# Nine diffusions instead of six ahead of the first blocks, in one step of a graph network's third layer

## The chip, the cores and the metric

The kernel runs on one core of a Trainium2 chip. The metric is the device time of one execution in microseconds (us). The engines are TensorE (PE: matmuls and transposes), VectorE (DVE), ScalarE (ACT), GpSimd (POOL) and SyncE (SP, which here only issues DMAs). Each engine works through its own queue in order; semaphores hold an instruction until what it needs is there.

## The reference

Four graph layers run one after the other on 4096 nodes with 256 features each, and all of them use one 0/1 adjacency matrix `adj` (4096 x 4096). After each layer the result is added to its input and normalised. Only layer 2 matters here. It does the following, cut to what is needed:

```python
R = S + eye(N);  R = R / R.sum(-1, keepdims=True)      # S is adj
Z = 0;  Xf = X;  Xa = X
for n in range(2):                                      # two steps
    A = top_p_attention(Xa, W1, W2, W3)                 # softmax, cut to the nucleus of 0.9
    Xf = R @ Xf                                         # diffusion
    Xa = A @ Xa                                         # attention
    Z = Z + Xf @ U1[n].T + Xa @ U2[n].T
h = X + Z                                               # then layer norms
```

`top_p_attention` forms the scores `q @ k.T` of all pairs of nodes, takes the softmax of each row, and keeps of each row the largest probabilities whose sum, before each, is under 0.9 (the nucleus).

## The kernel before, in words

The 4096 rows are worked in 32 blocks of 128 (NB = 32). Each of the two steps of layer 2 has the same parts, all in the function `layer2`:

- `keys` transposes the features and makes queries and keys; `spreads` computes, row by row, the quantities from which a first guess of the nucleus's threshold is made.
- `scores(b)` (L904) makes the scores of block b on PE in chunks and ACT exponentiates them (L886) into one of three buffers `e0`, `e1`, `e2`, taken in turn, each 128 x 4096. DVE adds up the partial sums (L912). As there are three buffers, block b + 3 overwrites block b, once block b's attention has transposed it.
- `guessed(e, b, ...)` (L915) is mostly ACT: from the sum it guesses a threshold (L929), and for blocks from 2 on ACT counts above it in four passes (L955); out of this come the corrected threshold `c2` (L894) and others.
- `nucleus(...)` (L969) is DVE: it starts at L1003 with `c2`, counts above the threshold with `evaluate` (L901; two counts in the second step, one in the first) and corrects it each time with help of ACT (L985 to L997), then sweeps the row (L1033), takes the largest values (L1037), finds the cut, and writes zeros below it: the edges (L1084, eight instructions).
- `attention(dst, e, r)` (L1209) is PE: 32 transposes (L1215), which ACT copies out of PSUM (L1217), and 32 products with the features (L1220).
- `diffusion(step, b)` (L1234) calls `diffuse`: 33 matmuls (L153, L159) into the PSUM tile `ps_r`, of which there is one buffer, with eight loads of adjacency pieces of 256 KB each by SP into five buffers. ACT (L1229) and DVE (L1230) scale the sum out of PSUM.
- `close(step, b, two)` (L1254) multiplies diffusion and attention with the weights (`terms`: PE L1250, DVE L1252), and in the second step normalises the rows, for which DVE (L80, L81, L1270, L1271, L1274), POOL (L83, L84) and ACT (L894) take turns. In the second step `ahead3` then computes what layer 3 needs of the block (PE L1284).

Before the loop over the blocks, each step runs `scores(0)`, `guessed`, the nucleus of block 0, and then EARLY = 6 diffusions, of blocks 0 to 5, whose results ACT stores in DRAM (`ahead`, L1320). The scores of blocks 1 and 2 come in between. In the loop, iteration b does the attention and the close of block b, the scores and guess of block b + 2, the nucleus of block b + 1, and obtains the diffusion of block b + 1: read back from DRAM by SP (L1326) where it was computed ahead, else computed there.

This is the order in the program's text. A scheduler then sets the order of each engine's queue, by priority, when the kernel is built; instructions of several blocks are interleaved in each queue. That order is fixed when the kernel runs.

Of the kernel before, what the change touches and what calls it, by code (L numbers as in the profile page):

```python
# [46 lines left out]
def row_broadcast(v, n):  # L47

    return bass.AP(tensor=v.tensor, offset=v.offset, ap=[[0, P], [1, n]])


class Net:
# [653 lines left out]
    def layer2(self):  # L706
        nc, tc, NB, D, X, N = self.nc, self.tc, self.NB, self.D, self.X, self.N
        A = 64
        HALF = N // 2
        with ExitStack() as ctx:  # L710
# [143 lines left out]
            def spreads(mom, qs, qg):  # L854

                for g in range(NB // 4):
                    pg = psum.tile([P, 512], F32, name="ps_tp")
                    for q in range(4):
                        b = 4 * g + q
                        s = b * P // 512 % 2  # L860
                        other = slice((1 - s) * A, (2 - s) * A)
                        nc.tensor.matmul(pg[:, q * P:(q + 1) * P], qs[other, b * P:(b + 1) * P], mom[other, :P],
                                         start=True, stop=True)
                    pg = pg.rearrange("p (q m) -> p q m", q=4)
                    t = qg[:, g % 4 * 256:g % 4 * 256 + 256].rearrange("p (q m) -> p q m", q=4)
                    nc.scalar.copy(t, pg[:, :, :A])
                    nc.vector.tensor_mul(t, t, pg[:, :, A:])
                    nc.vector.tensor_reduce(hvar[:, 4 * g:4 * g + 4], t, AX.X, ALU.add)
                nc.vector.tensor_scalar_max(hvar, hvar, 1e-6)
                nc.scalar.activation(lnr, hvar, AF.Ln)  # L870
                nc.scalar.activation(spread, lnr, AF.Exp, scale=0.5)
                nc.scalar.activation(lnr, lnr, AF.Identity, scale=0.5, bias=cs[:, 0:1])
                nc.vector.tensor_scalar(hvar, hvar, 0.5, -0.7, op0=ALU.mult, op1=ALU.add)
                nc.vector.tensor_scalar_add(qsp, spread, QUANTILE[-1])
# [29 lines left out]
            def scores(b):  # L904

                q = work.tile([P, P], F32, name="q", bufs=2)
                nc.sync.dma_start(q, qd[:, b * P:(b + 1) * P])
                e = es[b % 3][:, :N]
                zp = small("zp", HALF // 512)
                product(q, e, sums=zp)  # L910
                Z = Zs[:, b:b + 1]
                nc.vector.tensor_reduce(Z, zp, AX.X, ALU.add)  # L912
                return e
# [295 lines left out]
            def attention(dst, e, r):  # L1209
                pa = ps1.tile([P, 512], F32, name="ps_a")  # L1210
                for g in range(NB // 4):
                    pt = psum.tile([P, 512], F32, name="ps_tp")
                    for k in range(4):
                        jc = 4 * g + k
                        nc.tensor.transpose(pt[:, k * P:(k + 1) * P], e[:, jc * P:(jc + 1) * P], self.ident)  # L1215
                    aT = work.tile([P, 512], F32, name="aT", bufs=2)
                    nc.scalar.copy(aT, pt)  # L1217
                    for k in range(4):
                        jc = 4 * g + k
                        nc.tensor.matmul(pa[:, :D], aT[:, k * P:(k + 1) * P], X[:, jc, :],  # L1220
                                         start=(jc == 0), stop=(jc == NB - 1))
                nc.scalar.mul(dst, pa[:, :D], r)
# [6 lines left out]
                nc.scalar.mul(dst, pr[:, D:], rdeg[:, at(b)])  # L1229
                nc.vector.scalar_tensor_tensor(dst, pr[:, :D], rdeg[:, at(b)], dst, op0=ALU.mult, op1=ALU.add)  # L1230

            EARLY = min(6, NB)

            def diffusion(step, b):  # L1234

                dif = work.tile([P, 1, D], F32, name="dif")
                diffuse(dif[:, 0], b)
                if step == 0:
                    part = work.tile([P, 2, D], F32R, name="part", bufs=1)
                    self.split(part, dif[:, 0])  # L1240
                    nc.scalar.dma_start(xfd[b], part.bitcast(F32))
                return dif
# [36 lines left out]
            def ahead3(b, h, last=False):  # L1279

                pz = ps1.tile([P, 512], F32, name="ps_r")
                xT = self.transposed(psum, work, h, "xT")
                for c in range(2):
                    nc.tensor.matmul(pz, xT[:, c, :], w3[:, c].rearrange("p k m -> p (k m)"),  # L1284
                                     start=(c == 0), stop=(c == 1))
                if last:
                    self.split(XD[:, b], pz[:, D:])
                else:
                    part = work.tile([P, 2, D], F32R, name="part", bufs=1)
                    self.split(part, pz[:, D:])  # L1290
                    nc.scalar.dma_start(xfd[at(b)].rearrange("o p s d -> (o p) s d"), part.bitcast(F32))
                nc.scalar.copy(h[:, 0], pz[:, :D])
                nc.scalar.dma_start(xo[at(b), :, 1].rearrange("o p d -> (o p) d"), h[:, 0])

            for step in range(2):
                if step == 1:
                    for b in range(0, NB, 4):
                        nc.sync.dma_start(X[:, b:b + 4, :], xad[b:b + 4].rearrange("b p d -> p b d"))
                for i, ut in enumerate((self.u1t, self.u2t)):
                    nc.scalar.dma_start(u[:, i], ut[step].rearrange("(c p) m -> p c m", p=P))  # L1300
                nc.scalar.dma_start(affine, row_broadcast((self.ln_b, self.ln_g)[step], D))

                nc.scalar.preload_act_table_set("natural_log_exp_and_others")
                found = keys(X)
                if step == 1:
                    for k in range(2):
                        nc.scalar.dma_start(w3[:, :, k], self.w3[k * D:(k + 1) * D].rearrange("(c p) m -> p c m", p=P))
                if step == 0:
                    for b in range(NB):
                        self.split(XD[:, b], X[:, b, :])  # L1310
                e = scores(0)
                spreads(*found)
                stage = {0: guessed(e, 0, ABOVE[step])}
                rs = {0: nucleus(*stage[0], evals=1 + step)}
                difs = {}

                for k in range(EARLY):
                    if k in (2, 4):
                        stage[k // 2] = guessed(scores(k // 2), k // 2, ABOVE[step])
                    nc.scalar.dma_start(ahead[k], diffusion(step, k)[:, 0])  # L1320

                def diffused(b):
                    if b >= EARLY:
                        return diffusion(step, b)
                    dif = work.tile([P, 1, D], F32, name="dif")
                    nc.sync.dma_start(dif[:, 0], ahead[b])  # L1326
                    return dif

                difs[0] = diffused(0)
                for b in range(NB):  # L1330
                    if b + 1 < NB:
                        rs[b + 1] = nucleus(*stage[b + 1], evals=1 + step) if b == 0 else None
                    last = b == NB - 1
                    e, r = stage.pop(b)[0], rs.pop(b)
                    if last:
                        if step == 1:
                            ahead3(b - 1, h)
                        mend(step, e, r)

                        n = NB - step  # L1340
                        for k in range(0, n, 4):
                            to = min(k + 4, n)
                            nc.sync.dma_start(XD[:, k:to].bitcast(F32), xfd[k:to].rearrange("b p s d -> p b s d"))
                    att = work.tile([P, 1, D], F32, name="att", bufs=1)
                    attention(att[:, 0], e, r)
                    if step == 1 and 0 < b < NB - 1:
                        ahead3(b - 1, h)
                    h = close(step, b, (difs.pop(b), att))
                    if step == 1 and last:
                        ahead3(b, h, last)  # L1350
                    if 3 <= b + 2 < NB:
                        stage[b + 2] = guessed(scores(b + 2), b + 2, ABOVE[step])
                    if b + 1 < NB:
                        if b:
                            rs[b + 1] = nucleus(*stage[b + 1], evals=1 + step)
                        difs[b + 1] = diffused(b + 1)
# [114 lines left out]
```

## Time and profile before

| | |
|---|---|
| time, median of 10 runs | 4506.37 us (4500.6 to 4509.62) |
| the profiled execution's own time | 4505.58 us |
| its span in the profile | 4503.9 us |
| busy in the span: PE / DVE / ACT / POOL | 94% / 74% / 61% / 7% |
| layer 2's second step, from its first count on DVE to its last close | 2949.7 to 4236.2 us |
| block 0's attention begins on PE | 3008.3 us |
| block 9's attention begins on PE | 3336.9 us |
| block 30's attention begins on PE | 4157.7 us |

All times inside the run are counted from the start of the span. A wait "A <- B" is idle time of A's engine just before A, put down to B, whose end came last. In the lists in order of time, "x8" is the number of instructions merged in one line; a product of 32-bit numbers counts twice.

### The profile page before, as it was taken

To read this page: it belongs to the slowest core of one execution; us is meant where nothing else is said; L and a number is where in the kernel's file an instruction comes from. 1 tells how busy PE (TensorE), PEld (TensorE's weight loads), DVE (VectorE), ACT (ScalarE), POOL (GpSimd) and SP (SyncE) were. 2 spreads that over 40 slices of the span, in tenths; PEclk is the share of its full clock that TensorE was granted. 3 is DMA by queue.
4 is the path that set the end of the run, shared out by engine and by line. 5 is a ranking of instruction groups with operands and counts; after the bars stand their busy time and mean duration, and the time that the engine had idled before them with its cause. 6 is when DMAs were issued, how large, how long until landed. Compare 5 with 4: busy or idle time off the path is not lost. (4 is left out here: it accounts for less than half of the span.)

```text
span 4503.9 us, 70573 instructions
## 1 busy us (share of the span) xinstructions
PE 4244.9 (94%) x25625; PEld 3414.7 (76%) x25625; DVE 3344.6 (74%) x7657; ACT 2762.2 (61%) x5501; POOL 315.4 (7%) x538
## 2 busy tenths in 40 slices
PE   8999989999997999999999999887999999999799
PEld 7899989999986876677777767665666666666587
DVE  7632259999994446977777777388989999989354
ACT  5533369998873235866666666257677777676232
POOL 0111100001102100000000000001000000000011
PEclk9999999999998999999999999999999999999899
DMA  4765553342215964022222222530122222222541
GB/s 132 222 198 178 177 201 105 96 140 64 85 39 200 385 237 142 26 75 87 81 79 80 79 81 87 197 119 30 39 79 76 80 79 80 67 70 77 190 141 47
DMA packets 277781, 523.51 MB, mean 116 GB/s; under 512 B 36774, under 2 KB 112294, under 8 KB 273318
## 3 DMA queue, kind: packets, MB, share of 16 engines
q1 hardware_dynamic: 179268, 356.20, 23.7%
q10 hardware_dynamic: 85282, 122.62, 8.0%
q0 software_dynamic: 12864, 39.99, 3.0%
q8 instruction: 207, 3.39, 0.3%
q14 instruction: 160, 1.31, 0.1%
HBM read 363.63 MB, written 155.06 MB: 115 GB/s over the span
## 5 line engine op out<-in xcount | busy, mean ns | idle before, releaser
L1220 PE MATMUL ps_a<-X,aT 128*128 128x256 f32 x4096 | 960.1, 386 | 29.0 <-ACT aT L1217 28.4
L1220 PEld LDWEIGHTS ps_a<-X,aT 128*128 128x128 f32 x4096 | 760.2, 190 | 293.8 <-ACT aT L1217 141.2
L272 PE MATMUL acc<-gm,gt 128*128 128x198 bf16 x8192 | 710.2, 250 | 38.5 <-issue 17.9
L272 PEld LDWEIGHTS <-gt 128*128 128x128 fp8e4 x8192 | 705.2, 98 | 43.5 <-issue 18.0
L264 ACT ACTIVATE sg<-lpb,nlc 128x1024 fp8e4<-128x1024 f32 x640 | 671.1, 1139 | 78.9 <-DVE gt L266 39.0
L479 PE MATMUL pz<-src,ar 128*128 128x264 f32 x4096 | 510.4, 287 | 11.7 <-DVE ar L469 8.6
L479 PEld LDWEIGHTS pz<-src,ar 128*128 128x128 f32 x4096 | 506.6, 189 | 15.3 <-DVE ar L469 13.2
L159 PE MATMUL ps_r<-XD,adj_piece 128*128 128x512 f32 x2048 | 508.2, 400 | 10.1 <-DMA adj_piece<-adjs 9.9
L1217 ACT COPY aT<-ps_tp 128x512 f32<-128x512 f32 x512 | 277.8, 584 | 355.4 <-PE ps_tp L1215 350.4
L955 ACT ACTIVATE ja<-e,nc 128x2048 uint8<-128x2048 f32 x240 | 479.2, 1997 | 0.5 <-issue 0.2
L882 PE MATMUL ps_logit<-kT,q 64*128 64x512 f32 x1024 | 462.5, 637 | 4.0 <-ACT e L886 3.9
L159 PEld LDWEIGHTS ps_r<-XD,adj_piece 128*128 128x128 f32 x2048 | 382.9, 190 | 108.2 <-DMA adj_piece<-adjs 22.1
L901 DVE SCALAR_TENSOR_TENSOR v<-e,c 128x4096 bf16<-128x4096 f32 x100 | 447.3, 4473 | 7.3 <-ACT c L929 6.5
L1037 DVE MAX8 cand<-v 128x8 f32<-128x256 f32 x1024 | 360.9, 413 | 2.2
L1084 DVE SCALAR_TENSOR_TENSOR e<-e,edge 128x512 f32<-128x512 f32 x512 | 347.4, 747 | 1.5
L182 ACT ACTIVATE adj_piece<-na 128x1024 fp32r<-128x1024 fp8e4 x128 | 135.4, 1061 | 327.3 <-PE ps_adj L695 134.7
L472 ACT ACTIVATE nb<-a 128x512 uint8<-128x512 f32 x256 | 156.9, 632 | 292.4 <-DMA a<-in_adjt_dram 281.0
L1215 PE MATMUL ps_tp<-ident,e 128*128 128x128 f32 x2048 | 273.5, 275 | 39.2 <-DVE e L1084 26.1
L1033 DVE SCALAR_TENSOR_TENSOR v<-e,hi 128x2048 f32<-128x2048 f32 x128 | 301.0, 2351 | 1.7
L1215 PEld LDWEIGHTS ps_tp<-ident,e 128*128 128x128 f32 x2048 | 242.5, 142 | 78.0 <-DVE e L1084 29.5
L886 ACT ACTIVATE e<-ps_logit 128x1024 f32<-128x1024 f32 x256 | 261.4, 1022 | 48.5 <-PE ps_logit L882 33.6
L257 DVE TENSOR_SCALAR sg<-lpb,nlc 128x1024 fp8e4<-128x1024 f32 x384 | 274.2, 752 | 1.7
(301 smaller groups left out, 5093.4 us busy)
## 6 DMA issues: line engine op xcount, KB each, us to landing
adj_piece<-adjs SPq DMA_DIRECT2D x512, 256.0 KB
a<-in_adjt_dram SPq DMA_DIRECT2D x256, 256.0 KB
adjs<-adj_piece SPq DMA_DIRECT2D x128, 512.0 KB
na<-nad SPq DMA_DIRECT2D x64, 512.0 KB
na<-nad ACTq DMA_DIRECT2D x32, 1024.0 KB
nad<-nb POOLq DMA_DIRECT2D x128, 128.0 KB, 3.4
lpb<-lpd POOLq DMA_DIRECT2D x32, 512.0 KB, 4.2
xfd<-part ACTq DMA_DIRECT2D x63, 256.0 KB
```

The lines of the kernel that those rows point to most:

```text
L159: nc.tensor.matmul(ps, a[:, k, :], rhs(jc).rearrange("p s d -> p (s d)"), start=(jc == 0 and own is None), stop=(jc == self.NB - 1))
L264: nc.scalar.activation(sg[:, k, :], lpb, AF.Sign, scale=-1.0, bias=nlc[:, jc, h:h + 1], saturate=False)
L272: nc.tensor.matmul(acc[:, q, :6 * C1], gt[:, k, q * P:(q + 1) * P], gm[:, jc, hh, :], start=(jc == 0 and q % 2 == 0), stop=(jc == NB - 1 a ...
L479: nc.tensor.matmul(pz[q][:, t, :W], ar[:, q, k, :], src[:, jc, t, s], start=(jc == 0 and s == 0), stop=(jc == NB - 1 and s == 1))
L882: nc.tensor.matmul(pl[:, s, :], q[s * A:(s + 1) * A, :], kT[s * A:(s + 1) * A, c * 512:(c + 1) * 512], start=True, stop=True)
L901: nc.vector.scalar_tensor_tensor(junk, e, c, e, op0=ALU.is_ge, op1=ALU.mult, accum_out=S)
L955: nc.scalar.activation(ja, e[:, s * HALF:(s + 1) * HALF], f, bias=nc1, accum_out=fs[:, i + s:i + s + 1])
L1033: nc.vector.scalar_tensor_tensor(v, ec, hi, ec, op0=ALU.is_lt, op1=ALU.mult, accum_out=sb[:, s:s + 1])
L1037: nc.vector.max(cand[:, 8 * j:8 * j + 8], v[:, k * 256:(k + 1) * 256])
L1084: nc.vector.scalar_tensor_tensor(ec, ec, edge[:, j:j + 1], ec, op0=ALU.is_ge, op1=ALU.mult)
L1215: nc.tensor.transpose(pt[:, k * P:(k + 1) * P], e[:, jc * P:(jc + 1) * P], self.ident)
L1220: nc.tensor.matmul(pa[:, :D], aT[:, k * P:(k + 1) * P], X[:, jc, :], start=(jc == 0), stop=(jc == NB - 1))
```

## The change

In the second step nine diffusions (blocks 0 to 8) are made ahead of the block loop, not six (blocks 0 to 5). The first step keeps its six. The store to and the reload from DRAM go with each of the three; the loop no longer computes diffusions 6, 7 and 8.

```diff
-            EARLY = min(6, NB)
+            EARLY = min(9, NB)
...
-                for k in range(EARLY):
+                early = EARLY if step else min(6, NB)
+                for k in range(early):
                     if k in (2, 4):
                         stage[k // 2] = guessed(scores(k // 2), k // 2, ABOVE[step])
                     nc.scalar.dma_start(ahead[k], diffusion(step, k)[:, 0])

                 def diffused(b):
-                    if b >= EARLY:
+                    if b >= early:
                         return diffusion(step, b)
                     dif = work.tile([P, 1, D], F32, name="dif")
                     nc.sync.dma_start(dif[:, 0], ahead[b])
```

## The prediction

> **What bounds the kernel now.** I read the table of busy time by stretch first, to place layer 2's second step; then the waits inside the step, to see which engine waits for which; then the order of time on TensorE (PE) and VectorE (DVE) at the start of the block loop.
>
> The table by stretch of time, for seven stretches of the second step (columns: stretch, its length, then busy time of PE, PE's weight loads, DVE, ScalarE (ACT) and GpSimd (POOL), granted clock, DMA share, GB/s):
>
> ```profile
> 2949.00:3008.00 59.00, 46.88 (x185) 31.73 (x184) 56.90 (x118) 37.08 (x118) 0.00 (x0) 0.91 0.51 167
> 3008.00:3036.00 28.00, 27.76 (x126) 19.64 (x124) 26.79 (x78) 13.86 (x36) 0.00 (x0) 1.00 0.16 50
> 3036.00:3133.00 97.00, 88.39 (x392) 60.53 (x390) 80.34 (x213) 77.16 (x203) 11.84 (x12) 1.00 0.10 31
> 3133.00:3159.00 26.00, 0.32 (x1) 0.00 (x0) 25.21 (x78) 16.38 (x43) 1.72 (x4) 0.57 0.05 15
> 3159.00:3227.00 68.00, 64.35 (x276) 45.28 (x276) 66.44 (x175) 43.56 (x115) 2.06 (x4) 0.97 0.06 20
> 3227.00:3345.00 118.00, 115.29 (x495) 81.07 (x496) 105.22 (x283) 83.96 (x218) 9.49 (x12) 1.00 0.23 76
> 3345.00:4190.00 845.00, 813.33 (x3515) 576.35 (x3514) 781.17 (x2066) 583.37 (x1504) 42.65 (x88) 1.00 0.23 77
> ```
>
> Up to 3159 DVE is nearly always busy and PE has holes, one of 26 us; from 3227, where the loop's own diffusions begin, PE is busy 96 to 98%.
>
> The waits of PE and of DVE from 3000 to 4190 (total us, times, longest):
>
> ```profile
> PE ps_tp L1215 <- DVE e L1084: 25.8, 1, 25.8
> PE ps_a L1220 <- ACT aT L1217: 22.0, 35, 2.3
> PE ps_r L159 <- DMA adj_piece<-adjs: 8.8, 15, 1.2
> ```
> ```profile
> DVE c L1003 <- ACT c L894: 18.5, 5, 7.5
> DVE d L994 <- ACT gw L988: 9.6, 1, 9.6
> ```
>
> In the whole loop PE waits once for a nucleus (edges, L1084): before block 4's attention. From there to the end of the step no wait of PE is above 1.4 us, and blocks begin every 39.1 us (block 9's attention starts at 3336.9, block 30's at 4157.7). So the path is DVE up to 3159 and PE after it, and the end of the step moves with the LAST time that PE waits for DVE.
>
> PE, DVE and ACT in order of time (start, length, instruction, idle before it):
>
> ```profile
> 3018.68 1.04 PE L1215 MATMUL ps_tp<-ident,e 128*128 128x128 f32 x8
> 3036.50 1.11 PE L1215 MATMUL ps_tp<-ident,e 128*128 128x128 f32 x8
> 3159.15 1.97 PE L1215 MATMUL ps_tp<-ident,e 128*128 128x128 f32 x8 [25.83 <-DVE e L1084]
> 3160.94 5.09 PE L1220 MATMUL ps_a<-X,aT 128*128 128x256 f32 x16
> 3165.87 1.04 PE L1215 MATMUL ps_tp<-ident,e 128*128 128x128 f32 x8
> ```
> ```profile
> 3033.34 0.15 DVE L912 TENSOR_REDUCE Zs<-zp 128x1 f32<-128x4 f32 x1
> 3056.53 0.15 DVE L1003 SCALAR_TENSOR_TENSOR c<-c,c 128x1 f32<-128x1 f32 x1
> 3056.82 4.47 DVE L901 SCALAR_TENSOR_TENSOR v<-e,c 128x4096 bf16<-128x4096 f32 x1
> ```
> ```profile
> 3054.32 0.39 ACT L894 ACTIVATE c<-S,c,ri 128x1 f32<-128x1 f32 x1
> ```
>
> Block 3's scores are summed at 3033.34, ACT's guess for it is ready at 3054.32 + 0.39 = 3054.7, and DVE starts block 3's nucleus at 3056.5: two microseconds of slack.
>
> **The change part by part.** *PE.* A diffusion is 33 matmuls in 8.0 us (3262.54 to 3270.50). Three move ahead: 23.9 us of PE, none added. Six were already ahead, and they fill PE until block 0's edges come at 3003.6. In the changed program the new three therefore do not stand in PE's hole at 3133; they stand inside block 0's attention, one within its first quarter and two within its second. Each needs the one PSUM bank that its predecessor leaves through ACT (L1229) and DVE (L1230). The first runs 3009.8 to 3017.7. The second follows the DVE drain that stands behind the count at 3016.6 + 4.5: 3021.6 to 3029.6. The third's drain stands behind L1024 (3030.4): 3031.5 to 3039.5. Block 0's third quarter starts at 3040.7, not 3018.7: 22.0 us late.
>
> *DVE, block 3's nucleus.* The last pieces of block 3's scores stand behind these diffusions on PE, because they overwrite block 0's probabilities. Its sum moves from 3033.3 to 3055.4. From sum to guess ACT took 21.4 us; now 22.8, because the layer norm of block 0, late with its attention, stands between ACT's four passes. Guess: 3078.2. DVE meanwhile finishes block 2's nucleus. Before, that and block 0's layer norm were done at 3067.8, with 5.4 us of block 3's nucleus and block 0's third-layer rows between; three drains at 0.4 come in: 3067.8 - 5.4 + 1.2 = 3063.6. DVE waits 3078.2 - 3063.6 = 14.6 us; I take 14. Ends: 0 if the guess still came in time, 22 if nothing were left to do meanwhile.
>
> *DVE, the wait at L994.* Before, block 4's third count waited 9.6 + 1.8 us for ACT, whose queue held two of the next block's passes first. In the changed queues the like stands in block 3: its third correction waits behind block 1's close and four passes of block 4. By the same rows 4.0 for the close and 8.3 for the passes, 12.3 against 11.4: +1. Ends: -11 (gone) and +11 (both).
>
> *DVE order.* Summing the rows' durations in queue order, 16.4 us more of DVE work stands ahead of block 9's edges: both counts (2 x 4.47) and the first sweep (2.35) of block 10 and a close. Work, not idle; it only puts those edges later. Before, block 9's edges ended at 3326.3; now 3326.3 + 14 + 1 + 16.4 = 3357.7. PE starts an attention 4.6 us before the edges end (3159.15 against 3163.74): 3353.1.
>
> *PE after that.* Without its diffusion a block is 28 to 33 us of PE (3008.3, 3036.5, 3069.2, 3102.1), so PE waits for DVE in blocks 3 to 8 and is idle when block 9's edges come. The 24 us saved in blocks 6 to 8 become idle time. Block 9's attention starts at 3353.1, not 3336.9: +16.2. From there the queue is as before, a diffusion in each block, at 39.1 us a block.
>
> *Cold start.* After the 25.83 us gap the first groups took 1.97 and 5.09 us where others take 1.04 and 3.72, with the granted clock at 0.57 in the gap's stretch: 2.3 us. This now falls at block 9, on the path: +2.3. Earlier gaps cost nothing, as DVE is the path there. Ends: 0 and 2.3.
>
> The Trainium skill ("TensorE: Matmul & The Clock Gate", Part 1) says that after an idle window of about 3.4 us PE runs at half clock until 3.4 us of work have passed: an estimate from that page is 1.7 us for each gap, and this speaks against a change that makes several gaps of one. By the page the sum would be 0.6 us lower than by the row, which is used.
>
> *Queues.* ACT issues three more stores of 128 KB and SP three more loads (0.33 us of issue each). A store waits for DVE's drain with ACT behind it; for the third, ACT stands until 3041.1, before the aT copies, whose transposes end only at 3041.7: nothing. On SP the reload for block 0 now stands behind the adjacency pieces, which free up until 3039.5, and PE wants it at 3052. The adjacency moved at 167 GB/s while six ran, with 0.3 us of waiting: cover enough. If it were gone, 1.2 us for a late piece (longest wait above). POOL issues nothing of it. The first step keeps its six; the other layers are untouched.
>
> Sum: +16.2 + 2.3 = +18.5 us on the profiled execution's own 4505.58 us, which is 0.8 below the median of the ten runs (left out, being less than the rest is known to): **4524 us**.
>
> **The rivals.**
> *Relief in full (faster).* The moved 24 us go into the 26 us hole, and PE reaches block 9 earlier. For it: PE is at 96 to 98% from 3227 on, and DVE's later waits for ACT (18.5) would shrink too. Against it: two microseconds of slack at block 3's guess, and a queue that doesn't stop at the hole. Block 9's attention starts at 3326.3 - 11.4 + 16.4 - 4.6 = 3326.7 plus the two ACT waits together; the forecast has 26.4 of them (14 + 12.4), and at 10.2 the start is the old 3336.9: below that PE gains. With none it starts 10.2 early, without a cold start: 4495. The floor, all the moved PE work saved: 4482.
>
> The Trainium skill ("Perfetto Trace Analysis", Identifying the Most-Contended Engine) has the engine of highest occupancy optimised first; PE has 94% of the span and DVE 74%, so by that reading moving PE work into PE's hole brings the 24 us. The stretches above differ: up to 3159 it is DVE that is full.
>
> *No change that can be measured.* The two waits are half as long, 13: the start is 3339.7, +2.8, and the cold start 2.3: 4511. The same evidence as for relief, half heeded; against it, both waits follow from fixed queue orders.
>
> *Both ACT waits stay (slower still).* Block 4's 11.4 comes on top of block 3's: 18.5 + 11.4 = +30: 4536. For it: in before, DVE also waited 7.5 us for a guess at 3333, shortly after the block pattern changed; another such gives 4543.
>
> **How the numbers follow.** Against no change a measurement of this kernel can tell about 0.2%, 9 us. Forecast, +10 to +25: 0.53. Both waits: 0.15. No change: 0.19. Relief: 0.13. Slower 0.53 + 0.15 = 0.68. The range reaches down into the no-change case and up to both waits with the further one: 4500 to 4543; the forecast's own is 4515 to 4531.
>
> **What would show it.** In the profile of the changed kernel: three groups of L159 matmuls between 3008 and 3042; a DVE wait at L1003 for ACT L894 of about 14 us between 3060 and 3080; a wait of 4 to 12 at L997 some 20 to 30 us later; several waits of L1215 for L1084 in blocks 3 to 9 in place of one; block 9's attention at about 3353; 39.1 us a block after it. The prediction is wrong if L1003 finds its guess ready, if ACT's passes for block 3 run ahead of the late layer norm, or if PE still waits for nothing after block 5.

## The result, and the profile after

The changed kernel took 4523.48 us (median of 8 runs, 4519.55 to 4527.31) against 4506.49 us before (28 runs, 4497.40 to 4513.27): a ratio of 1.0039, 95% interval 1.0030 to 1.0047, or 17 us slower. Its profiled execution took 4518.24 us, span 4516.5, at a granted clock of 0.979 (before: 4505.58, 4503.9, 0.98). So the two profiled executions are 12.7 us apart where the medians are 17.0 apart; times inside the step are therefore also counted from the end of block 0's edges (the last L1084 of block 0: 3003.6 before, 3001.4 after), which takes out what differs ahead of the step.

The table by stretch of time, three of the same seven stretches (stretch, length, busy time of PE, PE's weight loads, DVE, ACT and POOL, granted clock, DMA share, GB/s):

```profile
...
3036.00:3133.00 97.00, 79.66 (x350) 54.63 (x348) 66.54 (x182) 68.53 (x174) 5.41 (x12) 0.95 0.13 42
3133.00:3159.00 26.00, 25.04 (x105) 19.22 (x106) 24.37 (x62) 13.65 (x39) 0.00 (x0) 0.86 0.00 1
...
3227.00:3345.00 118.00, 93.93 (x394) 64.44 (x392) 105.09 (x270) 84.18 (x233) 14.17 (x12) 0.90 0.08 24
...
```

Look at 3036 to 3133 first: DVE is busy 66.5 us where it was busy 80.3. The engine that carried this stretch now has 30 us of idle time. Then at 3227 to 3345: PE falls from 115.3 to 93.9 us, the three diffusions that it no longer has there. DVE is as busy as it was, so the time that PE saved is not passed on. The old hole at 3133 is full, but not with the moved work: block 3's attention has come later and lies there (it starts at 3133.5, before at 3102.1).

The waits of PE and then of DVE from 3000 to 4190 (total us, times, longest):

```profile
PE ps_tp L1215 <- DVE e L1084: 36.0, 4, 15.1
```

```profile
DVE c L1003 <- ACT c L894: 27.9, 6, 14.2
...
DVE d L994 <- ACT gw L988: 2.9, 4, 1.1
```

PE waits for nuclei four times in place of once. The wait for adjacency pieces is about what it was (10.0 us in all against 8.8). DVE's wait for a guess has a new longest, 14.2, and of the waits at L994, where the longest was 9.6, none is above 1.1.

In order of time, the instructions that the prediction named (start, length, instruction, idle before it):

```profile
3007.74 7.60 PE L159 MATMUL ps_r<-XD,adj_piece 128*128 128x512 f32 x32
3020.55 7.61 PE L159 MATMUL ps_r<-XD,adj_piece 128*128 128x512 f32 x32
3029.59 7.60 PE L159 MATMUL ps_r<-XD,adj_piece 128*128 128x512 f32 x32
...
3133.49 1.97 PE L1215 MATMUL ps_tp<-ident,e 128*128 128x128 f32 x8 [12.81 <-DVE e L1084]
...
3319.82 1.97 PE L1215 MATMUL ps_tp<-ident,e 128*128 128x128 f32 x8 [15.05 <-DVE e L1084]
```

```profile
3076.03 0.16 DVE L1003 SCALAR_TENSOR_TENSOR c<-c,c 128x1 f32<-128x1 f32 x1 [14.21 <-ACT c L894]
3090.99 0.42 DVE L1252 TENSOR_TENSOR h<-xb,ps_r 128x256 f32<-128x256 f32 x1 [3.21 <-PE ps_r L1250]
3102.97 0.16 DVE L997 TENSOR_TENSOR ri<-sq,d 128x1 f32<-128x1 f32 x1 [7.29 <-ACT sq L990]
```

```profile
3075.61 0.39 ACT L894 ACTIVATE c<-S,c,ri 128x1 f32<-128x1 f32 x1
```

This is the chain, link by link. Three diffusions stand on PE between 3007.7 and 3037.2, inside block 0's attention. ACT does block 0's layer norm at 3061.86 and has block 3's guess at 3075.61 + 0.39 = 3076.0. DVE starts block 3's nucleus at 3076.03, after 14.21 us of nothing. PE then waits 12.8 for block 3's edges, 5.2 for block 4's, 2.9 for block 7's and, last, 15.05 for block 8's, at 3319.8. Before, block 8's attention started at 3297.9.

### The profile page after: what moved, and what is told of

It reads as the page before. It is cut to its first block, busy times and chain, and to the rows that moved or that the text cites. A ratio compares the mean times of both kernels' runs of the same rounds, so it can differ in the third digit from the quotient of the medians.

```text
span 4516.5 us, 70581 instructions
## 1 busy us (share of the span) xinstructions
PE 4244.2 (94%) x25625; PEld 3416.3 (76%) x25625; DVE 3340.8 (74%) x7657; ACT 2761.1 (61%) x5501; POOL 310.4 (7%) x538
## 5 line engine op out<-in xcount | busy, mean ns | idle before, releaser
L479 PEld LDWEIGHTS pz<-src,ar 128*128 128x128 f32 x4096 | 504.0, 188 | 18.8 <-DVE ar L469 14.2
L955 ACT ACTIVATE ja<-e,nc 128x2048 uint8<-128x2048 f32 x240 | 479.2, 1997 | 1.8 <-DVE c L1019 1.1
L882 PE MATMUL ps_logit<-kT,q 64*128 64x512 f32 x1024 | 463.3, 637 | 3.8 <-ACT e L886 3.6
L901 DVE SCALAR_TENSOR_TENSOR v<-e,c 128x4096 bf16<-128x4096 f32 x100 | 447.3, 4473 | 7.3 <-ACT c L929 6.5
L1084 DVE SCALAR_TENSOR_TENSOR e<-e,edge 128x512 f32<-128x512 f32 x512 | 348.6, 746 | 1.4
L1033 DVE SCALAR_TENSOR_TENSOR v<-e,hi 128x2048 f32<-128x2048 f32 x128 | 300.9, 2351 | 1.8
L886 ACT ACTIVATE e<-ps_logit 128x1024 f32<-128x1024 f32 x256 | 261.4, 1022 | 53.4 <-PE ps_logit L882 39.1
```

Source lines behind the costliest of these rows:

```text
L479: nc.tensor.matmul(pz[q][:, t, :W], ar[:, q, k, :], src[:, jc, t, s], start=(jc == 0 and s == 0), stop=(jc == NB - 1 and s == 1))
L882: nc.tensor.matmul(pl[:, s, :], q[s * A:(s + 1) * A, :], kT[s * A:(s + 1) * A, c * 512:(c + 1) * 512], start=True, stop=True)
L901: nc.vector.scalar_tensor_tensor(junk, e, c, e, op0=ALU.is_ge, op1=ALU.mult, accum_out=S)
L955: nc.scalar.activation(ja, e[:, s * HALF:(s + 1) * HALF], f, bias=nc1, accum_out=fs[:, i + s:i + s + 1])
L1033: nc.vector.scalar_tensor_tensor(v, ec, hi, ec, op0=ALU.is_lt, op1=ALU.mult, accum_out=sb[:, s:s + 1])
L1084: nc.vector.scalar_tensor_tensor(ec, ec, edge[:, j:j + 1], ec, op0=ALU.is_ge, op1=ALU.mult)
```

## The experiments

**Theory 1**, the prediction's: the three diffusions stand inside block 0's attention and make block 3's guess late; DVE, which carries the step there, waits; what PE saves in blocks 6 to 8 turns into idle time. **Rivals**: the moved loads, stores and drains cost the time, not PE's; any extra diffusion has a fixed price, because it changes the order on the engines; the saving in blocks 6 to 8 is worth nothing wherever the work goes. **Theory 2** was formed on the way: DVE, and its waits behind ACT's queue, carry the step beyond block 4 too, nearly as much as PE does.

All runs, with the ratio of the time to before, and from each run's trace the time from the end of block 0's edges to the close (the start of L1252) of block 14 and of block 31. The last two columns are of one execution each, which can lie some microseconds from the median:

| kernel | time / before [95%] | us | to block 14 | to block 31 |
|---|---|---|---|---|
| before | | | 575.7 | 1232.5 |
| after (nine ahead) | 1.0039 [1.0030, 1.0047] | 4523.5 | 589.0 | 1248.1 |
| add3 | 1.0052 [1.0039, 1.0066] | 4528.0 | 590.4 | 1252.4 |
| pe3 | 1.0030 [1.0018, 1.0043] | 4518.7 | 589.7 | 1251.7 |
| free3 | 1.0003 [0.9994, 1.0012] | 4504.9 | 572.6 | 1236.2 |
| hole3 | 0.9995 [0.9986, 1.0004] | 4502.5 | 570.9 | 1228.3 |
| early7 | 0.9965 [0.9951, 0.9978] | 4492.9 | 561.0 | 1221.4 |
| early8 | 1.0048 [1.0034, 1.0062] | 4527.3 | 573.9 | 1260.3 |
| freeall | 0.9934 [0.9920, 0.9947] | 4477.3 | 568.8 | 1205.4 |
| chain4 | 0.9978 [0.9969, 0.9987] | 4498.2 | 563.2 | 1224.3 |
| add1 | 1.0032 [1.0022, 1.0042] | 4522.0 | 561.4 | 1249.7 |
| after0 | 1.0023 [1.0014, 1.0032] | 4518.0 | 588.3 | 1244.8 |
| after_c3 | 1.0011 [1.0002, 1.0020] | 4512.6 | 583.0 | 1242.0 |
| hole3c | 0.9985 [0.9976, 0.9994] | 4499.6 | 568.5 | 1226.0 |

Diffs are against the changed kernel unless it says otherwise.

### add3: the cost without the relief

```diff
                 def diffused(b):
-                    if b >= early:
+                    if b >= 6:
                         return diffusion(step, b)
```

> Nine diffusions ahead, as in the changed kernel, but the loop computes blocks 6 to 8 again as well: the cost of the move without its relief. Theory 1 (the three diffusions stand in block 0's attention and make block 3's nucleus late; what PE saves in blocks 6 to 8 becomes idle time): the relief was worth almost nothing, so about as slow as the changed kernel, +13 to +24 us on before (4520 to 4530), with the 14 us wait at L1003 unchanged; block 4's attention is 13 us later than before (3172) and PE then runs its full work at 39.1 us a block. Rival (the saving is real and only outweighed): the changed kernel's time plus 24 us, about +41 us (4547).

Measured: 4527.96 us, ratio 1.0052. DVE's wait at L1003 is there almost to the hundredth, and PE's waits for nuclei fall from four, 36.0 us, to two, 18.4 us:

```profile
3081.94 0.16 DVE L1003 SCALAR_TENSOR_TENSOR c<-c,c 128x1 f32<-128x1 f32 x1 [14.19 <-ACT c L894]
```

Doing the three diffusions twice costs 1.0052 - 1.0039 = 0.0013, about 6 us, more than doing them once (4.3 us by the last column). The intervals overlap: by their ends the difference lies between nothing and 0.0036, or 16 us. Of the 24 us that the change saves PE in blocks 6 to 8, then, about 4 to 6 count, and in no case all. The rival with a full 24 falls.

### pe3: PE's time alone

```diff
-                early = EARLY if step else min(6, NB)
+                early = min(6, NB)
...
+                for k in range(3 * step):
+                    pr = ps1.tile([P, 512], F32, name="ps_r")
+                    for jc in range(NB + 1):
+                        nc.tensor.matmul(pr, identr, XD[:, jc % NB].rearrange("p s d -> p (s d)"),
+                                         start=(jc == 0), stop=(jc == NB))
```

> Six diffusions ahead, as before, and after them, in the second step, three times 33 matmuls on data that lies in SBUF (extra work: no loads, no drains, no stores; nothing reads the result); the loop computes blocks 6 to 8 as before. Theory 1 (the PE time inside block 0's attention): PE's third quarter of block 0 is 24 us late, the wait at L1003 is there with 10 to 18 us, and the time is that of the run that adds three diffusions, +11 to +24 us (4518 to 4530). Rival queues (the moved loads, stores, reloads and drains cost the time, not PE's): the wait at L1003 is under 5 us and the time within 9 us of before (4498 to 4515).

Measured: 4518.73 us, ratio 1.0030. In order of time, the first of PE's three extra groups (the others follow it at 3019.1 and 3027.2) and DVE's waits in this kernel:

```profile
3010.95 8.05 PE L1326 MATMUL ps_r<-XD,identr 128*128 128x512 f32 x33
```

```profile
3079.67 0.16 DVE L1003 SCALAR_TENSOR_TENSOR c<-c,c 128x1 f32<-128x1 f32 x1 [14.19 <-ACT c L894]
...
3108.01 0.16 DVE L997 TENSOR_TENSOR ri<-sq,d 128x1 f32<-128x1 f32 x1 [8.72 <-ACT sq L990]
```

Matmuls that load, store and drain nothing make the same two waits, and to block 31 they cost 19.2 us where add3 costs 19.9. PE's time in that place is enough to make both waits, so the rival that puts the whole cost on loads, stores and drains falls. It may still have a part: the profiled execution of pe3 was the slowest of its six, and by the medians pe3 costs 0.0030 and add3 0.0052, with intervals that just touch. That leaves up to some 10 us open here; hole3, below, has the same loads, stores and drains as the changed kernel and is no slower than before.

### free3: the relief without the cost

```diff
-                early = EARLY if step else min(6, NB)
+                early = min(6, NB)
...
-                    if b >= early:
+                    if b >= (9 if step else early):
...
-                    nc.sync.dma_start(dif[:, 0], ahead[b])
+                    nc.sync.dma_start(dif[:, 0], ahead[b % 6])
```

> Six ahead, and blocks 6 to 8 of the second step take the stored diffusions of blocks 0 to 2 in place of their own: three diffusions are left out altogether, so this is the relief without its cost. Theory 1 says that relief was there to be had, if nothing stood ahead of block 3: DVE then carries the loop from block 4 to block 9; block 9's attention starts at 3320 instead of 3337 by DVE's own work, so -10 to -20 us (4486 to 4497). If DVE bound these blocks anyway (the rival that the saving in blocks 6 to 8 is worth nothing wherever the work goes): within 5 us of before (4501 to 4511).

Measured: 4504.87 us, ratio 1.0003: nothing. Theory 1 missed here; it had -10 to -20. A wait of DVE for ACT that before did not have comes up in block 8, and PE waits for that block. From the end of block 0's edges to the end of block 9's DVE is idle 14.7 us more than in before (40.2 against 25.5) and also busy 11.8 us more (309.0 against 297.2): its queue has more of the later blocks ahead of those edges. So the relief came with a cost of its own:

```profile
3278.24 0.16 DVE L997 TENSOR_TENSOR ri<-sq,d 128x1 f32<-128x1 f32 x1 [11.36 <-ACT sq L990]
```

```profile
3304.75 1.97 PE L1215 MATMUL ps_tp<-ident,e 128*128 128x128 f32 x8 [16.59 <-DVE e L1084]
```

And there was one place with little room in any case. Blocks 10 and 12 in before, DVE's edges:

```profile
3375.55 3.40 DVE L1084 SCALAR_TENSOR_TENSOR e<-e,edge 128x512 f32<-128x512 f32 x5
...
3440.03 5.39 DVE L1084 SCALAR_TENSOR_TENSOR e<-e,edge 128x512 f32<-128x512 f32 x8
```

and PE's attentions that take them:

```profile
3378.42 0.82 PE L1215 MATMUL ps_tp<-ident,e 128*128 128x128 f32 x6
...
3455.25 1.09 PE L1215 MATMUL ps_tp<-ident,e 128*128 128x128 f32 x8
```

PE shows no wait at block 10, but it comes only 2.9 us after the edges begin, and 2.1 us after the first of the eight ends. An engine that never waits can still have a neighbour right behind it. This is where Theory 2 comes from. Block 10 is the tightest place, though, and not the rule: at block 12, and at blocks 8, 9 and 11 to 30 alike, the first edge ends 13 to 28 us ahead of PE. There PE sets the pace in before, and DVE is faster only by about a microsecond a block: its edges come every 38.0 us from block 12 to block 16, where PE needs 39.1.

### hole3: the same diffusions, in PE's hole

```diff
-                early = EARLY if step else min(6, NB)
+                early = min(6, NB)
...
-                    if b >= early:
+                    if b >= (9 if step else early):
...
+                    for k in {3: (6, 7, 8)}.get(b, ()) if step else ():
+                        nc.scalar.dma_start(ahead[k], diffusion(step, k)[:, 0])
```

> Six ahead; the diffusions of blocks 6, 7 and 8 with their stores and reloads are issued after block 3, so they stand on PE just ahead of block 4's attention, in the hole of 26 us, with one drain each on ACT and DVE as in the changed kernel. Theory 1 (place on PE decides): no wait at L1003 for block 3 beyond 5 us, the hole filled, and faster than the changed kernel by 13 to 30 us: 4493 to 4510. Rival queues (loads, stores and drains of the moved ones cost it): as slow as the changed kernel, 4518 to 4530. Rival order (the scheduler puts a later block's counts ahead of block 9's edges in this order too, 16.5 us by the rows of before): 4515 to 4525, with the loss appearing only at block 9.

Measured: 4502.54 us, ratio 0.9995 [0.9986, 1.0004]: about 20 us faster than with the three inside block 0's attention, and no different from before. In order of time, the first of the three (the others at 3148.8 and 3159.4), and DVE's wait in block 4:

```profile
3137.71 7.58 PE L159 MATMUL ps_r<-XD,adj_piece 128*128 128x512 f32 x32
```

```profile
3126.00 0.22 DVE L994 SCALAR_TENSOR_TENSOR d<-S,S,gw 128x1 f32<-128x1 f32 x1 [9.57 <-ACT gw L988]
```

The hole is full, block 3's guess is in time, and DVE's wait in block 4, which made part of the hole (chain4, below), is what it was (9.57 + 1.84). So the place decides the cost, with the same loads, stores, drains and reloads; and even without a cost the 24 us that PE saves bring at most a few.

### after0: after block 0's attention

The diff is hole3's with `{0: (6, 7, 8)}` for `{3: (6, 7, 8)}`.

> Six ahead; the diffusions of blocks 6, 7 and 8 are issued after block 0's attention in place of inside it. Theory 1 (what stands in front of block 3's scores is what costs): DVE finds block 3's guess ready (wait at L1003 under 3 us there); the three now stand inside block 1's attention and make block 4's scores 16 to 24 us later, which meets the 11.4 us that DVE waits in block 4 anyway, so +3 to +12 us (4509 to 4518), less than with nine ahead. If every such place costs alike: +15 to +20.

Measured: 4517.98 us, ratio 1.0023. Block 3's guess is in time (its nucleus starts at 3054.7 without a wait). Block 1's attention is now the one that the three stand in (block 1 closes at 3090.4, before 3073.0), so the guess that is late is block 4's:

```profile
DVE c L1003 <- ACT c L894: 30.1, 4, 12.9
```

The 12.9 falls at 3112.9, in block 4. As Theory 1 has it, the three cost where they stand in front of a guess that DVE will soon want. Theory 1 also had it that one block further on they meet a wait that was there anyway and so cost less. That is not shown: the total is a little less (1.0023 against 1.0039), but up to block 14 they cost the same (588.3 against 589.0).

### early7 and early8: one at a time

```diff
-            EARLY = min(9, NB)
+            EARLY = min(7, NB)
```

> Seven diffusions ahead in the second step. Theory 1 (each one stands 8 us inside block 0's attention and so in front of block 3's guess, which had 2 us of slack and 3 us more from DVE's own later order): the wait at L1003 for block 3 is under 5 us, and the time within 6 us of before (4500 to 4511). Rival (a fixed price for any diffusion that goes beyond block 0's edges, because the order on the engines changes): +10 to +20 us, as with nine.

> Eight ahead. Theory 1: block 3's guess is 16 us later, DVE waits about 6 to 8 us for it, and the time lies between that of seven and that of nine: +6 to +14 us (4510 to 4519). Fixed price: +15 to +20.

Measured: seven 4492.94 us, ratio 0.9965; eight 4527.26 us, ratio 1.0048. Theory 1's times missed both, seven being faster than forecast and eight slower. Its waits held. Block 3's nucleus starts in the two kernels like this (seven first):

```profile
3064.80 0.16 DVE L1003 SCALAR_TENSOR_TENSOR c<-c,c 128x1 f32<-128x1 f32 x1
```

```profile
3070.36 0.16 DVE L1003 SCALAR_TENSOR_TENSOR c<-c,c 128x1 f32<-128x1 f32 x1 [8.17 <-ACT c L894]
```

With seven, eight and nine ahead the wait is 0, 8.2 and 14.2 us: the dose that Theory 1 asks for, and no fixed price. Up to block 14 the times follow it: 561.0, 573.9, 589.0. But the totals do not, for two reasons.

With seven the order on DVE has changed so that block 4's correction does not wait behind ACT any more: L994 waits 0.2 us in all where it waited 9.6, and up to block 14 that kernel is 14.7 us ahead of before. chain4, below, takes out that wait by itself and is 12.5 us ahead there. So the wait accounts for most of what makes seven faster than before, by 0.0035 [0.0022, 0.0049], the fastest kernel here that leaves nothing out.

With eight the kernel is 1.8 us ahead of before up to block 14, and then the loop runs slower to the end: from block 18's close to block 28's it takes 404.0 us, against 391.0 in before, 390.2 in after and 390.0 with seven. The next run shows the same loop.

### add1: seven without the relief

```diff
-            EARLY = min(9, NB)
+            EARLY = min(7, NB)
...
-                    if b >= early:
+                    if b >= 6:
```

> Seven ahead, but block 6's diffusion is computed again in the loop: the seventh without its relief. If the gain of seven (about -15 us) comes from the order on the engines (DVE's wait of 9.6 + 1.8 us behind ACT in block 4 is gone), it stays: 4491 to 4500. If it comes from the 7.6 us that PE saves in block 6: 4501 to 4510.

Measured: 4522.01 us, ratio 1.0032; both expectations missed. Up to block 14 it is level with early7 (561.4 and 561.0), so the gain of seven is there without block 6's relief, and comes from the order. After that it is the slow loop again: 402.8 us from block 18's close to block 28's. In order of time, the first of these waits and one turn of the loop, on DVE:

```profile
3614.64 0.48 DVE L1230 SCALAR_TENSOR_TENSOR dif<-ps_r,rdeg,dif 128x256 f32<-128x256 f32 x1 [6.92 <-ACT dif L1229]
...
3978.26 4.47 DVE L901 SCALAR_TENSOR_TENSOR v<-e,c 128x4096 bf16<-128x4096 f32 x1
3982.65 0.48 DVE L1230 SCALAR_TENSOR_TENSOR dif<-ps_r,rdeg,dif 128x256 f32<-128x256 f32 x1
3984.59 4.46 DVE L901 SCALAR_TENSOR_TENSOR v<-e,c 128x4096 bf16<-128x4096 f32 x1
```

Here DVE's queue has the drain of a diffusion (L1230) between or just ahead of a nucleus's two counts (L901), and has to wait for it; in before, and in after in the same blocks, the drain stands behind the two sweeps (L1033). In this kernel and in early8 DVE waits 25.0 and 23.3 us for L1229 where it waits 0.5 in before. In both, PE starts nearly every attention within 0.1 us of its block's first edge (blocks 19 to 30 with eight, 17 to 30 in add1), where before has 18 us or more in these blocks. So in the slow loop DVE sets the pace, and in the other PE does. No run moves the drain by itself, so that its place makes the loop slow is read from the traces and not shown. What makes the scheduler settle into the one loop or the other was not found either: one diffusion more or less in the early blocks is enough to tip it, and it shows only at blocks 16 to 19, first as a wait of 11.5 us at L122 for ACT (L121).

### freeall: PE's work taken out

```diff
-                early = EARLY if step else min(6, NB)
+                early = min(6, NB)
...
-                    if b >= early:
+                    if b >= (NB if step else early):
...
-                    nc.sync.dma_start(dif[:, 0], ahead[b])
+                    nc.sync.dma_start(dif[:, 0], ahead[b % 6])
```

> Six ahead, and every later block of the second step takes one of the six stored diffusions in place of its own: 26 diffusions, 198 us of PE's work and their adjacency loads, are left out altogether. Theory 2, formed after the run that left out three without a gain (DVE carries the step nearly as much as PE does: its edges come every 38.1 us where PE needs 39.1, and block 10's edges start 2.9 us before PE takes them): -10 to -45 us (4460 to 4495). If PE bounded the step from block 4 on, as the prediction has it, PE would need 31.5 us for a block and DVE at most the 36 us that it is busy: -80 us or more (under 4425).

Measured: 4477.25 us, ratio 0.9934, some 30 us. Of PE's waits:

```profile
PE ps_tp L1215 <- DVE e L1084: 170.0, 14, 26.0
```

198 us of work are gone from PE, and its waits for DVE's nuclei rise from 25.8 us to 170.0: 144 of the 198 come back as waits. So PE does not carry this step alone, though it is busy 96 to 98% of it from 3227 on in before. That high share says that PE is full, not that DVE has room.

### chain4, after_c3, hole3c: DVE's wait for ACT

Against the kernel before (chain4, `b in (4,)`), the changed kernel (after_c3, `b in (3,)`) and hole3 (hole3c, `b in (4,)`); lines below it stand 6 lower than in the others:

```diff
                     nc.vector.reciprocal(ic, c)
+                    if evals == 2 and k == 3 and b in (4,):
+                        nc.vector.scalar_tensor_tensor(gw, S0, thr, ic, op0=ALU.subtract, op1=ALU.mult)
+                        nc.vector.tensor_mul(sq, gw, gw)
+                        nc.vector.tensor_mul(gw, gw, ic)
+                        nc.vector.scalar_tensor_tensor(sq, sq, 400.0, ri, op0=ALU.add, op1=ALU.mult)
+                    else:
                         nc.scalar.mul(gw, g0, ic)
```

> Before, with four small steps (L986 to L990) of block 4's third correction in the second step moved from ACT to DVE, four instructions of 0.15 to 0.2 us, so that DVE does not wait behind ACT's passes there (9.6 + 1.8 us in before). Theory 2 (waits of DVE for ACT's queue set the time of this step): the 25.8 us hole of PE shrinks by about 11 and the time falls by 3 to 11 us (4493 to 4501), less if another wait for ACT comes in its place. If the wait was hidden: within 2 us of before.

> The changed kernel, with the four small steps of block 3's third correction in the second step moved from ACT to DVE (as was done for block 4 in the kernel before). Theory 1: the wait of 14 us at L1003 stays, for it is a guess that is late; the wait of 7.3 us at L997 goes, and the time falls by 3 to 8 us against the changed kernel (4514 to 4521). If the loss were in the order alone and not in the waits: no difference to the changed kernel.

> Both at once: the three diffusions after block 3, and block 4's third correction on DVE. Theory 2 (DVE and its waits for ACT set this step, the relief of PE is worth nothing): like the kernel before with that correction alone, 4494 to 4502. If the relief counts once DVE is not held up: 4480 to 4492.

Measured: chain4 4498.18 us, ratio 0.9978; after_c3 4512.63 (Theory 1 had 4514 to 4521), ratio 1.0011, against 1.0039 for the changed kernel without it; hole3c 4499.60, ratio 0.9985. One block's five small instructions on ACT, done as four on DVE, are worth 10 us in before and about 13 in the changed kernel (6 by the last column). In chain4 PE's longest wait for a nucleus falls from 25.8 to 10.1 us.

In after_c3 the late guess stays (14.2 us) and the wait of the correction is gone; another one, of 8.5, has come up two blocks on, at L994's counterpart:

```profile
DVE d L1000 <- ACT gw L994: 11.0, 3, 8.5
```

And hole3c is no faster than chain4: with DVE less held up in block 4, moving three diffusions into what is left of the hole still brings nothing. That fits Theory 2, but does not isolate it: hole3c has two other waits of DVE for ACT, of 7.2 and 6.1 us, up to block 10.

## Why the prediction was right, step by step

The forecast was 4524 us and slower; it came out at 4523.5, and by the chain that it described. Two of its terms were off, in opposite directions, so that the total came out this close is luck in part. It is luck too that nine ahead kept the loop's pace of before: eight ahead did not, and the forecast had no term for that.

*PE.* Right: the three were to start at 3009.8, 3021.6 and 3031.5; their matmuls start at 3007.7, 3020.6 and 3029.6, with block 0's third quarter at 3039.2 (forecast 3040.7).

*DVE, block 3's nucleus.* Right: 14 us forecast, 14.21 measured, at 3076.0 (forecast 3078.2). Block 3's scores are summed at 3053.5 (forecast 3055.4), and the guess is ready 22.5 us later (forecast 22.8). pe3 shows that PE's time alone makes it, early7 and early8 that it grows with each diffusion once the slack is used up.

*DVE, the wait at L994.* Right in kind: L994 in block 4 no longer waits, and L997 in block 3 does. Its size was 12.3 forecast, 7.29 measured; the 4.0 for block 1's close show up as 3.21 at L1252, 12 us ahead of it. Together 10.5 for the old 11.4, so -1 where +1 was forecast. after_c3 confirms that it counts.

*DVE order.* Right: 16.4 us more work forecast ahead of the end of block 9's edges; from the end of block 0's edges to there DVE is busy 314.2 us where it was busy 297.2: 17.0.

Those terms add up to block 9's edges ending at 3357.7; they end at 3364.6, in an execution that reached block 0's edges 2.2 us earlier. The missing part is idle time of DVE: up to there it rose from 25.5 to 49.0, 23.5 where 15 was forecast, some of it in three waits of 1.7 to 1.8 us ahead of block 8's edges (L1252, L1003 and L997 between 3273 and 3290).

*PE after that.* **This is the step that failed**, in two ways that nearly cancelled. The last wait of PE was to be at block 9, 16.2 us late. It is at block 8, at 3319.8: 21.9 late by the clock, 24.1 counted from block 0's edges. And "from there the queue is as before" does not hold: block 8's own diffusion stands at 3300.3 in before, behind the start of that block's attention (3297.9), and in after it is gone. Block 9's attention, forecast at 3353.1, starts at 3365.1, now behind that block's own diffusion (3355.4); and from there to block 30's attention a block takes 38.3 us, not 39.1. From block 8's attention to block 14's close PE is busy 272.4 us before and 262.3 after, with seven diffusions against six and 124 against 108 score matmuls (L882). So the relief of block 8 was not lost, as the step had it for all three; 24.1 - 10.7 leaves 13.3 at block 14's close (rounded), and 15.6 at block 31's. add3 gives the same relief from the other side, 4 to 6 us.

*Cold start.* Right: 2.3 forecast. At block 8 the first group takes 1.97 for 1.04, and the next 4.85 for 3.72, so about 2.1 in all:

```profile
3322.26 4.85 PE L1220 MATMUL ps_a<-X,aT 128*128 128x256 f32 x16 [0.46 <-ACT aT L1217]
```

The Trainium skill ("TensorE: Matmul & The Clock Gate", Part 1) speaks of an idle window of about 3.4 us. The gaps of 5.2, 12.8 and 15.05 us before 2.11, 1.97 and 1.97 agree with that. Shorter ones do not: after 2.92 us (3269.6, block 7) four instructions took 1.08, where eight take 1.04, and with seven ahead the group after 3.07 us (3145.4) took 2.11. So here a gap somewhat shorter than the page's is enough.

*Queues.* Right as far as the traces go: pe3, without any of them, and add3, with all of them, cost 19.2 and 19.9 us to block 31. By the medians up to some 10 us stay open, as said there.

*The rival "relief in full"* was priced at 4495 with a floor of 4482, on the condition that DVE did not wait for ACT. No run meets that condition: free3 has the relief, takes 4504.9, and DVE waits for ACT in blocks 4 and 8; hole3c has no such wait in block 4, but two others, and takes 4499.6. The reading behind the price, "DVE up to 3159 and PE after it", was too sharp. From 3036 to 3133 PE was the busier of the two (88.4 of 97 us, DVE 80.3). The statement that PE had no wait above 1.4 us from block 4 to the end overlooked one of 2.3 at 3199.8, for ACT, and one of 6.1 ahead of block 31's attention. And nobody looked at how close behind DVE's edges PE came: 2.9 us at block 10. freeall shows how little a full relief can bring, 198 us out of PE for 30. The Trainium skill ("Perfetto Trace Analysis", Identifying the Most-Contended Engine) has the engine of highest occupancy optimised first, but has the headroom of TensorE judged by the share of its peak or by its weight loads, and not by its busy matmuls. The 94% of PE that the prediction set against DVE's 74% are busy matmuls. By weight loads PE has 76% of the span, close to even, and in the stretch from 3345 to 4190 before it has 576 of 845 us against 781 on DVE. chain4 agrees with that: four instructions moved to DVE from the queue that it waited for gained a third as much as freeall.

*"No change"* and *"both ACT waits stay"* did not come about: the first wait was not half as long, and block 4's did go.

## What to carry to other kernels

Work that goes ahead of a loop is not free because the loop has a hole: find where the queue really puts it, and which later start has the least slack behind that place; here it was a guess three blocks on, with two microseconds. Before counting a relief, look at how far ahead of their use the next engine's results arrive, block by block, and at how fast that engine could go by itself, not only at whether anyone waits: an engine at 97%, with a feeder that is faster by only a microsecond in 39, has little to give. And where a scheduler orders the queues, try the neighbouring values too: seven, eight and nine ahead gave 0.9965, 1.0048 and 1.0039.

## What was not expected of the hardware and the queues

One loop body ran at two paces: 39.1 us a block (391.0 for ten) or 40.4 (404.0). What the traces show to differ is the order of DVE's queue, with a drain of 0.48 us between or just ahead of the counts in the slower one.

Five small instructions of one block, done as four of 0.15 to 0.2 us on DVE, were worth 10 us (0.9978): on ACT they stood behind passes of 2.0 us each (L955) of the next block.

A 128x1 addition on POOL took twenty times as long where it met one of DVE's counts. In order of time, in the kernel before:

```profile
3108.36 4.47 DVE L901 SCALAR_TENSOR_TENSOR v<-e,c 128x4096 bf16<-128x4096 f32 x1
...
3108.42 4.48 POOL L83 TENSOR_SCALAR ln_var<-ln_mv 128x1 f32<-128x1 f32 x1 [1.34 <-DVE ln_mv L81]
```

The same instruction takes 0.22 us in 52 of its 69 executions in this step before. Here it begins with the count and ends with it, and five others that begin with a sweep of 2.35 us (L1033) take 2.29. ACT's small steps were moved to DVE in the runs above and not to POOL, idle as that is; POOL was not tried.
